# A four-layer graph attention kernel: order of emission, values by Strassen, lengths by a power

## The chip, the core and the metric

The kernel runs on one core of one Trainium2 chip. A core has five engines, each with its own queue of instructions: TensorE (PE, matrix products, results into PSUM), VectorE (DVE), ScalarE (ACT, functions by table and copies), GpSimd (POOL) and SyncE (SP, which here issues transfers). They run side by side and wait for one another by semaphores. The metric is the device time of one execution in microseconds (us), taken as the median of the runs.

## What is computed

128 graphs of 64 nodes with 512 features go through four layers. Each layer normalizes, applies ReLU, and adds the result of a masked attention to its input. Layers 0 and 2 have four heads of 64, layer 1 has eight and a second normalization. Layer 3 multiplies its attention by a second mask, the pairs of nodes whose cosine is over 0.1, and for this it needs the length of each head's vector at each node. The reference, cut:

```python
# layers 0 and 2 (x is the normalized input, 512 wide; q, k, v are 256 wide)
q, k, v = split_heads(x @ Wq), split_heads(x @ Wk), split_heads(x @ Wv)
sim = jnp.where(adjacency_mask[:, None], jnp.einsum('bhid,bhjd->bhij', q, k) * scale, neg)
out = jnp.einsum('bhij,bhjd->bhid', jax.nn.softmax(sim, axis=-1), v)   # then @ Wo + bo
# layer 1: the same with 8 heads, q, k, v and output 512 x 512
# layer 3
m = embs @ map_w.T + map_b
sem = m.reshape(b, s, h, dk).transpose(0, 2, 1, 3)
norm = jnp.maximum(jnp.linalg.norm(sem, axis=-1, keepdims=True), COS_EPS)
n = sem / norm
cos_adj = (einsum('bhsd,bhtd->bhst', n, n) * keep > THRESHOLD)
# q and k from m, softmax as above
adj = cos_adj * p_attn
Ax = jnp.einsum('hbst,hbtd->hbsd', adj_h, embs @ gcn_map_w.T + gcn_map_b)
out = jax.nn.relu(Ax @ gcn_W.T / (adj_h.sum(-1, keepdims=True) + 1.0))
```

## The kernel before

The work is cut into 16 steps of 512 rows (eight graphs) for each layer. The kernel is written as streams: Python generators that say, ahead of each instruction, which engine it needs and for how long (`yield act(0.6)` for 0.6 us of ScalarE). While the program is built, an object `Order` steps through all streams as if they ran, and emits each next instruction from the stream that could start first. These figures therefore decide the order in which instructions stand on each engine; they have no other effect. Buffers come from rings and banks, and a stream that asks for one waits until the earlier user has let go.

```python
def run(self):
    while self.live:
        ...
        s = min(self.live, key=lambda s: (s.start(self.free), s.prio))
        eng, dur, lat = s.op
        at = s.start(self.free)
        self.free[eng] = at + dur
        s.ready = at + dur + lat
        s.last = (eng, at + dur)
        self.step(s)
```

Almost all 512 x 512 products are done by Winograd's form of Strassen's method: both operands are cut into quarters, sums of quarters are made, and seven products of quarters take the place of eight. `A` holds the weights with their sums (made once by GpSimd), `B` the quarters of the tokens and `T` their sums (four GpSimd instructions a step). A product of quarters is four matmuls (two halves of 128, two steps of contraction). Three PSUM banks are used in turn; each product's result must be copied out or added before its bank takes the next:

```python
def product(bank, A, B, tokens_out, first):
    KC = A.shape[1]
    for m in range(2):
        o = bank[:, m * H:(m + 1) * H]                # H = 256
        for k in range(KC):
            yield pe(0.432)
            ...
            nc.tensor.matmul(o, l, r, ...)

def winograd(A, BT, tokens_out, out_, used, begun):
    ...                                               # "first": copy by ACT; "second": add by DVE
    mA = product(A[:, 0], B(0, 0)); read, c11 = first(0, 0, mA)
    mB = product(A[:, 1], B(1, 0)); c11 = second(0, 0, mB, c11)
    wait read;  mA = product(A[:, 5], T[:, 1]); read, u2 = first(0, 1, mA)
    mC = product(A[:, 4], T[:, 0]); read5, c22 = first(1, 1, mC)
    wait read;  mA += product(A[:, 2], T[:, 2]); read, c22 = add(1, 1, mA, c22)
    wait read5; mC += product(A[:, 6], B(1, 1)); c12 = second(0, 1, mC, u2)
    wait read;  mA += product(A[:, 3], T[:, 3]); alone(1, 0, mA)
```

(This last function is shortened to its order.) The values of layers 0 and 2 are the exception, plain products of 512 x 256:

```python
def v_proj(inT, w, t):
    n = w.shape[2]                                    # 256
    p_, e = yield from r_mm.new("mmv")
    for c in range(NC):                               # NC = 4
        yield pe(0.857 * n / 512)
        nc.tensor.matmul(p_[:, 0:n], inT[:, c, t * P:(t + 1) * P], w[:, c, :], ...)
    return p_[:, 0:n], e
...
for t in range(TB):                                   # TB = 4
    p_, e = yield from v_proj(h, v_part(W[f"vo{l}"]), t)
    od.spawn(evict(V[:, t, 0:D // 2], p_, e), 0)      # one copy by ACT
```

The lengths of layer 3 (the four rows of `mmn` matmuls sum the squares; only 8 of the 128 rows of `rs` are of use):

```python
def norms(mT, s, m_ready, ready, used):
    ...                                               # squares by ACT, sums by PE into p_
    nc.vector.tensor_scalar_max(rs, p_, 1e-16)
    nc.scalar.activation(rs, rs, AF.Sqrt)
    for h in range(4):
        v = rs[:, h * P:(h + 1) * P]
        nc.vector.reciprocal(v, v)
    nc.sync.dma_start(d, rs)                          # d is in DRAM
    for c in range(NC):
        for par in range(2):                          # each row spread over 64 partitions
            nc.sync.dma_start(t[par * N:(par + 1) * N, :], ...d[32 * c + par]...)
    yield used                                        # q and k of this step are done with mT
    for c in range(NC):
        nc.gpsimd.tensor_mul(mT[:, c, :], mT[:, c, :], t)
    ready.set()                                       # now the scores of mT with itself
```

Of the kernel before, what the change touches and what calls it, by code (L numbers as in the profile page):

```python
# [43 lines left out]

class Event:
# [38 lines left out]


class Order:


    def __init__(self):
        self.live, self.free, self.now, self.held = [], {}, 0.0, set()  # L90

# [28 lines left out]

    def run(self):
        while self.live:
            new = [s for s in self.live if s.op is None]
            if new:
                self.step(new[0])
                continue
            s = min(self.live, key=lambda s: (s.start(self.free), s.prio))
            eng, dur, lat = s.op
            at = s.start(self.free)
            self.free[eng] = at + dur  # L130
            s.ready = at + dur + lat
            s.last = (eng, at + dur)
            self.step(s)
        assert not self.held, [where(s.gen) for s in self.held]
# [51 lines left out]

def dve(us):
# [11 lines left out]
def load(us=2.2):  # L199
    return ("sp", 0.35, us)  # L200
# [3 lines left out]
def gnn_stack(ctx: ExitStack, tc: tile.TileContext, a: dict, out: bass.AP):  # L204
# [80 lines left out]
    def v_part(t):  # L285

        return t.rearrange("p a k n -> p (a k) n")[:, 0:4]

    def o_part(t):

        return t.rearrange("p a k n -> p (a k) n")[:, 4:11, None, :]

    def wo_halves(t, n):
# [4 lines left out]
             ("vo0", lambda t: [(a["Wv0"], v_part(t))] + wo_halves(t, "Wo0")),  # L298
# [3 lines left out]
             ("vo2", lambda t: [(a["Wv2"], v_part(t))] + wo_halves(t, "Wo2")),  # L302
             ("map3", lambda t: halves(t, "map3")), ("sem3", lambda t: []),
             ("q3", lambda t: halves(t, "q3")), ("k3", lambda t: halves(t, "k3"))]
    for key, _ in units:
        w_ready[key], w_sums[key] = od.event(), od.event()
    bo, bo_done = {}, {}

    def sums_of_a(A):

        for o, i0, i1, op in ((4, 2, 3, ALU.add), (5, 4, 0, ALU.subtract),
                              (6, 1, 5, ALU.subtract), (2, 0, 2, ALU.subtract)):
            yield pool(1.3)
            nc.gpsimd.tensor_tensor(A[:, o], A[:, i0], A[:, i1], op)

    def sums_of_b(B, T, vector=False):

        n = T.shape[2]
        for o, i0, i1 in ((T[:, 0], B(0, 1), B(0, 0)), (T[:, 1], B(1, 1), T[:, 0]),
                          (T[:, 2], B(1, 1), B(0, 1)), (T[:, 3], B(1, 0), T[:, 1])):  # L320
            if vector:
                yield dve(0.6 * n)
                nc.vector.tensor_tensor(o, i0, i1, ALU.subtract)
            else:
                yield pool(0.65 * n)
                nc.gpsimd.tensor_tensor(o, i0, i1, ALU.subtract)  # L326

    def weights():
        for key, parts in units:
# [17 lines left out]
            yield from sums_of_a(o_part(t) if key in ("vo0", "vo2") else t)  # L347
# [36 lines left out]
    def scales(v):  # L384
# [13 lines left out]
        yield dve(0.2)  # L398
# [4 lines left out]
    def normalize(v, rs, func):  # L403
        for t in range(2):
            yield act(0.69)
# [11 lines left out]
    def loads(steps):  # L417
        for l, s in steps:
            if l > 0:
                yield x_done[l - 1, s]  # L420
            for half in range(2):
                v, e = yield from r_xin.new()
                loaded[l, s, half] = v, e
                yield load()
# [80 lines left out]
    def product(bank, A, B, tokens_out, first):  # L505

        KC = A.shape[1]
        for m in range(2):
            o = bank[:, m * H:(m + 1) * H]
            for k in range(KC):  # L510
                yield pe(0.432)
                if tokens_out:
                    l, r = B[:, k, m * P:(m + 1) * P], A[:, k, :]
                else:
                    l, r = A[:, k, m * P:(m + 1) * P], B[:, k, :]
                nc.tensor.matmul(o, l, r, start=(first and m == 0 and k == 0),  # L516
                                 stop=(k == KC - 1), skip_group_check=True)

    class Out:
# [5 lines left out]
        def first(self, i, k, p_, read, done):  # L525
# [4 lines left out]
            else:  # L530
                for m in range(2):
                    yield act(0.45)
# [5 lines left out]
        def second(self, i, k, p_, after, done):  # L538
            yield after
            o = self.view(i, k)  # L540
            yield dve(0.69)
# [3 lines left out]
        def add(self, i, k, p_, after, read, done):  # L545
# [6 lines left out]
            yield dve(0.7)  # L552
# [3 lines left out]
        def alone(self, i, k, p_, done):  # L556
            yield from self.first(i, k, p_, done, od.event())

    def winograd(A, BT, tokens_out, out_, used, begun):

        B, T, *sums = BT

# [3 lines left out]
        def first(i, k, p_):  # L566
            read, done = ev(2)
            od.spawn(out_.first(i, k, p_, read, done), 0)
            return read, done

        def second(i, k, p_, after):
            done = od.event()
            od.spawn(out_.second(i, k, p_, after, done), 0)
            return done

        def add(i, k, p_, after):
            read, done = ev(2)
            od.spawn(out_.add(i, k, p_, after, read, done), 0)
            return read, done

        p_, pe_ = yield from r_ma.new("mA")
        yield from product(p_, A[:, 0], B(0, 0), tokens_out, True)
        read, c11 = first(0, 0, p_)
        q_, qe = yield from r_mm.new("mB")
        yield from product(q_, A[:, 1], B(1, 0), tokens_out, True)
# [7 lines left out]
        r_, re_ = yield from r_mm.new("mC")  # L593
        yield from product(r_, A[:, 4], T[:, 0], tokens_out, True)
# [11 lines left out]
        od.spawn(out_.alone(1, 0, p_, pe_), 0)  # L606
        od.spawn(when([c11, c12, c22, pe_], used), 0)
# [41 lines left out]
    def evict(o, p_, e):  # L649
        yield act(0.4)  # L650
        nc.scalar.copy(o, p_)
        e.set()

    def v_proj(inT, w, t):
        n = w.shape[2]
        p_, e = yield from r_mm.new("mmv")
        for c in range(NC):
            yield pe(0.857 * n / 512)
            nc.tensor.matmul(p_[:, 0:n], inT[:, c, t * P:(t + 1) * P], w[:, c, :],  # L659
                             start=(c == 0), stop=(c == NC - 1))  # L660
        return p_[:, 0:n], e

    st, p_ready, s_ready, p_used, with_ones = {}, {}, {}, {}, []

    def projections(steps):
        for l, s in steps:
# [4 lines left out]
            if l in (0, 2):  # L671
# [3 lines left out]
                od.spawn(when([used], s_ready[l, s], t_done[l, s],  # L675
                              w_done[f"qk{l}"] if end else None), 0)
# [3 lines left out]
                es = [used]  # L680
                for t in range(TB):
                    p_, e = yield from v_proj(h, v_part(W[f"vo{l}"]), t)
                    od.spawn(evict(V[:, t, 0:D // 2], p_, e), 0)
                    es.append(e)
                z["v"] = V
                od.spawn(when(es, p_ready[l, s], h_done[l, s]), 0)
# [73 lines left out]
    def norms(mT, s, m_ready, ready, used):  # L760
# [14 lines left out]
        rs, re_ = yield from r_u.new("rs")  # L775

        yield dve(0.69)
        nc.vector.tensor_scalar_max(rs, p_, 1e-16)
        pe_.set()
        yield act(1.9)  # L780
        nc.scalar.activation(rs, rs, AF.Sqrt)
        for h in range(4):
            v = rs[:, h * P:(h + 1) * P]
            yield dve(0.87)
            nc.vector.reciprocal(v, v)
        d = dram.tile([P, TB * P], F32, name=f"rs{s}")
        yield load()
        nc.sync.dma_start(d, rs)
        re_.set()
        nr = []  # L790
        for c in range(NC):
            t, e = yield from r_u.new("nr")
            yield ("sp", 0.35, 1.0)
            for par in range(2):
                v = d[32 * c + par:32 * c + par + 1, :]
# [13 lines left out]
    def scores(lT, rT, npair, blocks):  # L809
# [3 lines left out]
        for b, t in enumerate(blocks):  # L813
            for ch in range(nch):
                j = ch * nb + b
                yield pe(0.29)
# [55 lines left out]
    def masks(l, s):  # L872
# [3 lines left out]
        yield load()  # L876
# [22 lines left out]
    def residuals(l, s, w_there, got):  # L899
        yield w_there  # L900
        for k in range(2):
            xr, xe = yield from r_xres.new()
            yield load()
# [8 lines left out]
    class Residual(Out):  # L912
# [26 lines left out]
        def alone(self, i, k, p_, done):  # L939
            return self.second(i, k, p_, None, done)  # L940

    def store(l, s, done, got, evs):
# [3 lines left out]
        for k in range(2):  # L946
            xr, xe = got[k]
            yield load()
# [10 lines left out]
    def attention(l, s):  # L959
# [8 lines left out]
        for u, blocks in enumerate(units):  # L968
# [3 lines left out]
            for b, t in enumerate(blocks):  # L972
                for ch in range(nch):
                    j = ch * per + b
                    yield pe(0.29)
# [224 lines left out]
```

## Time and profile before

| | before |
|---|---|
| median of 3 runs | 2981.0 us |
| lowest and highest | 2978.83 and 2983.35 us |
| span of the profiled execution | 2978.9 us |
| instructions | 63888 |

The profile is of one execution. For each engine it gives busy time and its share of the span; PEld is the loading of weights, which overlaps the matmuls. A group of instructions is one line of code with its tiles and shapes: busy us, mean ns of one, then the idle us of the engine just before them and who ended that wait. An f32 matmul is two records, a transpose is one. The chain of work that ended last is followed back from the end, and tells whose time the span is. A timeline line has the start, the length, the engine, the line of code and the tiles, the number of instructions merged, and in brackets the idle time before and who ended it. A wait line has the total us, the number of times and the longest.

| group in the page's fifth part | count | busy us | mean ns |
|---|---|---|---|
| L659 PE, plain products of the values | 1024 records | 233.4 | 380 |
| L516 PE, mA from t and w_q, one of the groups of Strassen products | 768 records | 187.1 | 379 |
| L785 DVE, reciprocals of the lengths | 64 | 57.1 | 917 |
| L397 POOL, power of the normalization, 128x2 | 160 | 118.4 | 740 |
| L757 POOL, row of gcn added | 64 | 81.4 | 1305 |

(The third row is from the list of all groups.)

### The profile page before, as it was taken

To read this page: it belongs to the slowest core of one execution; us is meant where nothing else is said; L and a number is where in the kernel's file an instruction comes from. 1 tells how busy PE (TensorE), PEld (TensorE's weight loads), DVE (VectorE), ACT (ScalarE), POOL (GpSimd) and SP (SyncE) were. 2 spreads that over 40 slices of the span, in tenths; PEclk is the share of its full clock that TensorE was granted. 3 is DMA by queue.
4 is the path that set the end of the run, shared out by engine and by line. 5 is a ranking of instruction groups with operands and counts; after the bars stand their busy time and mean duration, and the time that the engine had idled before them with its cause. 6 is when DMAs were issued, how large, how long until landed. Compare 5 with 4: busy or idle time off the path is not lost.

```text
span 2978.9 us, 63888 instructions
## 1 busy us (share of the span) xinstructions
PE 2910.6 (98%) x27176; PEld 2468.1 (83%) x27176; DVE 1727.3 (58%) x2748; ACT 1336.6 (45%) x2361; POOL 1465.2 (49%) x1144
## 2 busy tenths in 40 slices
PE   8999999999999999999999999999999999999997
PEld 6888888888888888888888888887888787888876
DVE  5665566664554555445456556556666666665566
ACT  4444445544444444433444444454444444444442
POOL 6666667444344334335566566663344343344332
PEclk9999999999999999999999999999999999999998
DMA  5323333211112112113233332422232222222212
GB/s 163 116 88 123 95 101 126 67 62 66 48 45 73 59 44 73 59 44 98 94 114 104 102 116 88 138 82 64 72 90 83 63 62 66 70 85 71 52 48 62
DMA packets 162957, 244.05 MB, mean 82 GB/s; under 512 B 17392, under 2 KB 69616, under 8 KB 162672
## 3 DMA queue, kind: packets, MB, share of 16 engines
q1 hardware_dynamic: 149760, 226.56, 24.3%
q10 hardware_dynamic: 12912, 13.42, 1.4%
q8 instruction: 213, 3.49, 0.5%
q14 instruction: 72, 0.59, 0.1%
HBM read 168.60 MB, written 71.30 MB: 81 GB/s over the span
## 4 chain that ended last, share of the span: by engine, by line
PE 85%; DVE 6%; ACT 4%; DMA 2%; POOL 2%; issue 1%; SPq 0%; DVEq 0%; ACTq 0%; POOLq 0%
PE mA L516 37%; PE mC L516 18%; PE mB L516 10%; PE sc L824 4%; PE mmv L659 4%; PE ptp L864 3%; PE ptr L477 3%; PE po L983 2%; ACT E L846 1%; PE po L1118 1%; DVE E L843 1%; DVE sc L835 1%; DVE mx L840 1%; PE mmn L773 1%; PE ptr L454 1%
## 5 line engine op out<-in xcount | busy, mean ns | idle before, releaser
L853 POOL TENSOR_TENSOR E<-E,sm 128x1024 f32<-128x1024 f32 x96 | 186.3, 1941 | 424.2 <-DVE sm L851 298.7
L390 DVE BATCH_NORM_STATS2 st<-xin 128x6 f32<-128x512 f32 x320 | 215.6, 674 | 260.2 <-DMA xin<-x 206.9
L929 POOL TENSOR_TENSOR xres<-xres,u 128x512 f32<-128x512 f32 x192 | 243.4, 1268 | 250.0 <-ACT u L924 245.0
L908 POOL TENSOR_TENSOR xres<-xres,u 128x512 f32<-128x512 f32 x192 | 257.7, 1365 | 219.5 <-DMA xres<-x 99.6
L406 ACT ACTIVATE xin<-xin,rs 128x512 f32<-128x512 f32 x320 | 243.7, 808 | 110.9 <-DVE rs L399 110.7
L397 POOL TENSOR_TENSOR rs<-rs,mhalf 128x2 f32<-128x2 f32 x160 | 118.4, 740 | 276.9 <-DVE rs L395 270.3
L659 PE MATMUL mmv<-w_vo,hT 128*128 128x256 f32 x1024 | 233.4, 380 | 0.9 <-DVE xres L542 0.9
L659 PEld LDWEIGHTS mmv<-w_vo,hT 128*128 128x128 f32 x1024 | 193.5, 190 | 29.0 <-DVE xres L542 2.6
L326 POOL TENSOR_TENSOR t<-hT 128x512 f32<-128x512 f32 x128 | 178.3, 1393 | 73.2 <-ACT hT L482 39.0
L326 POOL TENSOR_TENSOR t<-hT,t 128x512 f32<-128x512 f32 x128 | 172.3, 1346 | 50.5 <-ACT hT L459 46.6
L399 DVE SCALAR_TENSOR_TENSOR rs<-mv,rs 128x2 f32<-128x2 f32 x160 | 80.3, 502 | 197.7 <-POOL rs L397 197.7
L516 PE MATMUL mA<-t,w_qk 128*128 128x256 f32 x768 | 187.0, 380 | 2.8 <-ACT qk L529 2.5
L516 PE MATMUL mA<-t,w_k 128*128 128x256 f32 x768 | 182.7, 381 | 4.8 <-ACT kT L533 4.7
L516 PE MATMUL mA<-t,w_q 128*128 128x256 f32 x768 | 187.1, 379 | 0.0
L516 PEld LDWEIGHTS mA<-t,w_k 128*128 128x128 f32 x768 | 144.8, 190 | 28.2 <-ACT kT L533 8.3
L516 PEld LDWEIGHTS mA<-t,w_qk 128*128 128x128 f32 x768 | 143.1, 190 | 22.0 <-ACT qk L529 3.3
L868 ACT COPY pt<-ptp 128x512 f32<-128x512 f32 x192 | 112.7, 588 | 105.1 <-PE ptp L864 105.1
L516 PEld LDWEIGHTS mA<-t,w_q 128*128 128x128 f32 x768 | 143.1, 190 | 18.1
L849 DVE TENSOR_REDUCE sm<-E 128x16 f32<-128x1024 f32 x96 | 116.4, 1212 | 69.5 <-ACT E L846 69.5
L757 POOL TENSOR_TENSOR v<-v,gcn_row 128x512 f32<-128x512 f32 x64 | 81.4, 1305 | 150.4 <-ACT v L615 150.4
L482 ACT COPY hT<-ptr 128x512 f32<-128x512 f32 x192 | 113.7, 592 | 74.1 <-PE ptr L477 74.1
L846 ACT ACTIVATE E<-E 128x1024 f32<-128x1024 f32 x96 | 101.5, 1058 | 83.6 <-DVE E L843 83.3
(210 smaller groups left out, 6819.0 us busy)
## 6 DMA issues: line engine op xcount, KB each, us to landing
x<-xres SPq DMA_DIRECT2D x96, 512.0 KB, 3.8
xin<-x SPq DMA_DIRECT2D x96, 512.0 KB, 3.8
xres<-x SPq DMA_DIRECT2D x64, 512.0 KB, 4.2
xin<-in_x SPq DMA_DIRECT2D x32, 512.0 KB, 3.8
xres<-in_x SPq DMA_DIRECT2D x32, 512.0 KB, 4.6
u<-rs SPq DMA_DIRECT2D x128, 128.0 KB, 3.1
xres<-x SPq DMA_DIRECT2D x256, 64.0 KB, 2.3
out<-xres SPq DMA_DIRECT2D x256, 64.0 KB, 2.1
```

The lines of the kernel that those rows point to most:

```text
L326: nc.gpsimd.tensor_tensor(o, i0, i1, ALU.subtract)
L390: nc.vector.bn_stats(st, v[:, t, :])
L397: nc.gpsimd.tensor_tensor(rs[:, 0, :], rs[:, 1, :], mhalf[:, :2], ALU.pow)
L406: nc.scalar.activation(v[:, t, :], v[:, t, :], func, bias=rs[:, 2, t:t + 1], scale=rs[:, 0, t:t + 1])
L516: nc.tensor.matmul(o, l, r, start=(first and m == 0 and k == 0), stop=(k == KC - 1), skip_group_check=True)
L659: nc.tensor.matmul(p_[:, 0:n], inT[:, c, t * P:(t + 1) * P], w[:, c, :], start=(c == 0), stop=(c == NC - 1))
L824: nc.tensor.matmul(S[a_ * N:(a_ + 1) * N, par, col], lT[r, c, k], rT[r, c, k], start=True, stop=True)
L846: nc.scalar.activation(E, E, AF.Exp, scale=0.125)
L849: nc.vector.tensor_reduce(sm, E, AX.X, ALU.add)
L853: nc.gpsimd.tensor_mul(E, E, sm[:, :, None].to_broadcast([P, 16, N]))
L908: nc.gpsimd.tensor_add(xr[:, t, :], xr[:, t, :], bo[l])
L929: nc.gpsimd.tensor_add(v, v, both(u))
```

## The change

It has three parts. First, the values of layers 0 and 2 are computed by the same seven products as the rest, with quarters of the weights 128 columns wide; `v_proj` and its copy go. This is meant to take multiplications away. Second, the lengths of layer 3: the eight useful rows of sums go to DRAM and come back as 128 x 32, GpSimd raises them to the power -0.5, they go to DRAM and are spread as before. This takes away the root, whose table ACT has to load in place of that for Exp, and the reciprocals of 512 columns. Third, the order of emission: the assumed times are corrected, a change between 64-row matmuls ("quads") and full ones is charged 0.085 us, and a long ACT or DVE instruction of low priority gives way to an urgent one that could start within its time. Also the transfers at the end of layer 3 are written as two of 128 KB where there were four of 64 KB. The diff, cut to its core:

```diff
+DRAIN = 0.085
 class Order:
+    def urgent(self, s):
+        eng, end = s.op[0], s.start(self.free) + s.op[1] - 0.1
+        if s.prio <= 0 or eng not in ('act', 'dve'):
+            return None
+        r = [x for x in self.live if x.prio <= 0 and x.op is not None and x.op[0] == eng
+             and x.start(self.free) < end]
+        return min(r, key=lambda x: x.start(self.free), default=None)
     def run(self):
             s = min(self.live, key=lambda s: (s.start(self.free), s.prio))
-            eng, dur, lat = s.op
+            s = self.urgent(s) or s
+            eng, dur, lat = s.op[:3]
             at = s.start(self.free)
+            if eng == "pe":
+                at += DRAIN * (self.quads != s.quads())
+                self.quads = s.quads()
...
 def load(us=2.2):
-    return ("sp", 0.35, us)
+    return ("sp", 0.6, us)
...
     def normalize(v, rs, func):
-            yield act(0.69)
+            yield act(0.81)
...
     def product(bank, A, B, tokens_out, first):
-        KC = A.shape[1]
+        KC, n = A.shape[1], bank.shape[1] // 2
-            o = bank[:, m * H:(m + 1) * H]
+            o = bank[:, m * n:(m + 1) * n]
-                yield pe(0.432)
+                yield pe(max(0.219, 0.432 * n / H))
...
     def winograd(A, BT, tokens_out, out_, used, begun):
+        width = 2 * A.shape[3] if tokens_out else 2 * H
...                                                   # "used" now waits for every eviction
     def projections(steps):
-                for t in range(TB):
-                    p_, e = yield from v_proj(h, v_part(W[f"vo{l}"]), t)
-                    od.spawn(evict(V[:, t, 0:D // 2], p_, e), 0)
-                    es.append(e)
+                def vv(i, k, V=V):
+                    return V[:, 2 * k:2 * k + 2, i * P:(i + 1) * P]
+                es = [used, (yield from unit(v_part(W[f"vo{l}"]), (*BT, wv_sums[l]), True, Out(vv)))]
-                od.spawn(when(es, p_ready[l, s], h_done[l, s]), 0)
+                od.spawn(when(es, p_ready[l, s], t_done[l, s], h_done[l, s]), 0)
...
     def norms(mT, s, m_ready, ready, used):
-        nc.vector.tensor_scalar_max(rs, p_, 1e-16)
-        yield act(1.9)
-        nc.scalar.activation(rs, rs, AF.Sqrt)
-        for h in range(4):
-            v = rs[:, h * P:(h + 1) * P]
-            yield dve(0.87)
-            nc.vector.reciprocal(v, v)
-        nc.sync.dma_start(d, rs)
+        nc.vector.tensor_copy(ss, p_)
+        for c in range(NC):
+            nc.sync.dma_start(d[0][2 * c:2 * c + 2, :], ss[32 * c:32 * c + 2, :])
+        nc.sync.dma_start(rs, d[0].rearrange("h (k n) -> (h k) n", n=32))
+        nc.vector.tensor_scalar_max(rs, rs, 1e-16)
+        yield pool(6.0)
+        nc.gpsimd.tensor_tensor(rs, rs, mhalf[:, 0:1].to_broadcast([P, 32]), ALU.pow)
+        nc.sync.dma_start(d[1].rearrange("h (k n) -> (h k) n", n=32), rs)
...
     def scores(lT, rT, npair, blocks):
-                yield pe(0.29)
+                yield quads(0.235)
```

## The prediction

> **What bounds the kernel now.** I read the page's first two parts, then the chain, then the busy times by stage, then the timeline around waits of TensorE (PE). The stretches of the third fence are, roughly, layers 0 to 3.
>
> ```profile
> PE 2910.6 (98%) x27176; PEld 2468.1 (83%) x27176; DVE 1727.3 (58%) x2748; ACT 1336.6 (45%) x2361; POOL 1465.2 (49%) x1144
> PEclk9999999999999999999999999999999999999998
> ```
> ```profile
> PE 85%; DVE 6%; ACT 4%; DMA 2%; POOL 2%; issue 1%; SPq 0%; DVEq 0%; ACTq 0%; POOLq 0%
> ```
> ```profile
> 0.00:520.00 520.00, 498.37 (x4327) 426.35 (x4328) 309.75 (x511) 246.00 (x423) 337.17 (x276) 1.00 0.36 115
> 520.00:1470.00 950.00, 944.13 (x8471) 820.37 (x8469) 500.06 (x838) 419.84 (x649) 403.96 (x318) 1.00 0.20 66
> 1470.00:1955.00 485.00, 479.61 (x4130) 412.22 (x4131) 277.45 (x430) 223.07 (x397) 304.45 (x243) 1.00 0.31 105
> 1955.00:2979.00 1024.00, 988.48 (x10252) 809.14 (x10250) 640.06 (x970) 447.65 (x893) 419.60 (x310) 0.99 0.25 69
> ```
>
> The columns after the length of a stretch are busy us of PE, its weight loads, DVE, ACT and POOL. PE is the bound in every layer, at full clock; no other engine passes 70% of a stage. So only two things count: PE work taken out, and PE waits. Work saved on DVE, ACT, POOL or DMA counts only through such a wait.
>
> PE's real waits are partly inside its busy time. Matmul records start 0.216 us apart but last 0.38, so a wait under 0.16 us is not idle and a longer one shows 0.16 short. This is a wait in layer 3, PE first, then ACT at the same moment:
>
> ```profile
> 2252.72 1.89 PE L516 MATMUL mA<-t,w_map 128*128 128x256 f32 x8
> 2255.18 1.99 PE L516 MATMUL mC<-hT,w_map 128*128 128x256 f32 x8 [0.57 <-ACT m L533]
> ```
> ```profile
> 2252.05 1.28 ACT L846 ACT_TABLE_LOAD   x1
> 2253.34 1.06 ACT L846 ACTIVATE E<-E 128x1024 f32<-128x1024 f32 x1
> 2254.30 0.82 ACT L533 ACTIVATE m<-mC,vecs 128x256 f32<-128x256 f32 x2
> ```
>
> Eight records at 0.216 should have brought the next start at 2254.45; it came at 2255.18, 0.73 us late (0.57 shown). ACT copied bank mC late because it had reloaded a table for Exp, just as long as the wait could bear. The whole list of PE's waits for ACT begins:
>
> ```profile
> PE mC L516 <- ACT m L533: 8.6, 15, 0.6
> PE mC L516 <- ACT u L924: 6.2, 16, 0.5
> PE mA L516 <- ACT kT L533: 4.7, 4, 1.2
> ```
>
> With 0.16 us added to each, that is 11.0, 8.8 and 5.3 us. The three are most of what can be gained in the steady state; the start (first PE work at 9.69 us) and the last 20 us hold the rest.
>
> [...]The trace has two records of 0.216 us for one f32 matmul of 256 columns[...]; the groups show 16 loads at Sqrt and 16 at Exp of layer 3, 1283 ns each.[...]
>
> **Part 1, values by Strassen (layers 0 and 2).** Removed: 512 matmuls of 256 columns (16 for each of 32 steps), the 1024 records of this group:
>
> ```profile
> L659 PE MATMUL mmv<-w_vo,hT 128*128 128x256 f32 x1024 | 233.4, 380 | 0.9 <-DVE xres L542 0.9
> ```
>
> At start-to-start pace 1024 x 0.216 = 221 us (233.4 counts tails). Added: seven products of four matmuls, 28 x 32 = 896, each 128 columns wide; the built program has exactly these counts. Does such a matmul take half, or does loading 128x128 weights for only 128 columns bind? The fold of the weights, in the middle of the kernel, has that shape:
>
> ```profile
> 1492.74 0.81 PE L659 MATMUL mmv<-w_vo,hT 128*128 128x256 f32 x3
> 1493.39 1.05 PE L377 MATMUL mmf<-bdw,bb 128*128 128x128 f32 x8
> 1494.28 1.43 PE L659 MATMUL mmv<-w_vo,hT 128*128 128x256 f32 x5
> ```
>
> Eight records from 1493.39 to 1494.28: 0.89 us, 0.111 each, 0.222 for a matmul. So weight loads do not bind, and 896 x 0.222 = 199 us. PE saves 221 - 199 = 22 us.
>
> What it adds elsewhere: ACT has five 128x256 copies for four, at 0.37 us (47.0 us / 128 in the old group), +12 us; DVE has two adds from PSUM and one from SBUF a step, which layer 3's same lines show at 0.40 and 0.53 us, 32 x 1.33 = +43 us; POOL forms four weight sums of half width in each of the two layers, and holds T longer. All off the bound. The new danger is that a bank is reused after shorter products. In the new order mA is reused after a product on mC (0.89 us) and mostly a matmul of another unit (0.43): 1.3 us for tail (0.16), copy (0.37) and handover. That is enough unless ACT is inside a long instruction (Exp 1.06, output copy 1.01, normalize 0.81). I estimate 0.2 us a step, +6 us in all.
>
> **Part 2, lengths by a power.** Removed: 64 reciprocals (57 us of DVE), 16 roots (10 us) and, what matters, both table loads of each step, since Exp's table now stays. Without the 1.28 us before Exp, the copy of mC in the fence above comes 1.28 us earlier, against a wait of 0.73. The order of the map unit is otherwise unchanged there. Gain 11 us.
>
> Added: a trip to DRAM and back before the power, and the power on 128x32. The only power in the trace is small:
>
> ```profile
> L397 POOL TENSOR_TENSOR rs<-rs,mhalf 128x2 f32<-128x2 f32 x160 | 118.4, 740 | 276.9 <-DVE rs L395 270.3
> ```
>
> If nothing of the 0.74 us is fixed, 32 columns take 11.8 us; the scheduler's own figure in the changed source is 6.0. Is it on the path? In the step shown, the rows of gcn are added until 2227.2 on POOL, the lengths are first used by the scores of m at 2257.97, and the order puts the power right after these rows. After it come a store (about 2.8), eight broadcast reads (about 5 to issue, 3.1 to land: the page's DMA part) and four products of 5.4 in sum: 2227.2 + power + 16.3 = 2243.5 + power. So a power up to some 14 us costs nothing. Net 0.
>
> **Part 3, order of emission.** Both builds have the same 505 changes between 64-row and full-size PE work, so the new drain charge saves none. It does move work: in the output units of layers 0 and 2, mC's second use stood after one product (0.86 us) and waited for ACT's copy:
>
> ```profile
> 314.52 1.03 PE L516 MATMUL mA<-w_vo,t 128*128 128x256 f32 x4
> 316.05 1.13 PE L516 MATMUL mC<-w_vo,m 128*128 128x256 f32 x4 [0.51 <-ACT u L924]
> ```
>
> It now has a matmul of the next step in between, 1.3 us. I count 8 of 8.8 us. The rule that puts evictions ahead of other long work on ACT should take some of the kT waits, 4 of 5.3, and a few small waits at the removed matmuls, 2. I give back 5 us for waits that the order makes elsewhere and that I can't see.
>
> **Sum.** -22 (PE work) + 6 (V banks) - 11 (table loads) - 8 - 4 - 2 + 5 (order) = -36. 2981 - 36 = 2945 us, ratio 0.988.
>
> **Rivals.**
> *The V units stall.* Products of 0.89 us on three banks could each wait 0.3 us for ACT or DVE; at three a step that is 29 us instead of 6, and the time 2968. For: ACT and DVE get 55 us more in these layers, in the same moments. Against: 1.3 us between uses, and ACT below 50%.
> *The power is long.* At 20 us it passes the room of 14 by 6 us, sixteen times: +96 and 3041. For: 0.74 us for two columns is very slow. Against: even taken wholly as per-column it stays at 11.8.
> *Only arithmetic counts.* The new order brings nothing and the table wait is replaced by another: 2981 - 22 + 6 = 2965.
> *The order does more.* All three listed waits vanish, nothing new comes, and the end shortens by some us: 2981 - 22 - 25 - 8 = 2926.
>
> **Range and chances.** The arithmetic (-22) is nearly sure; the waits are not, each way by some 15 to 20 us. Eight in ten: 2924 to 2966. Faster by over 2% means below 2921.4, which needs more than every listed wait: 0.07. Slower by over 2% (above 3040.6) needs the long power or a broken pipeline: 0.03. Within 2%: 0.90.
>
> **What would show it.** PE records 27,944; 128-column records about 0.111 us apart; one table load left for Exp in the whole layer 3; no waits of mC at map for ACT m; waits at w_vo near zero; layer 1's pace of 57.0 us a step unchanged; a step of layer 0 some 1.2 us and of layer 3 some 0.8 us shorter. Wrong if scores of m wait for POOL's m products, if the power is over 14 us, or if new waits of mA and mC for ACT v sum to over 20 us.

## The result and the profile after

| | before | after |
|---|---|---|
| median | 2980.59 us (4 runs) | 2936.85 us (4 runs) |
| lowest and highest | | 2935.35 and 2939.24 us |
| span of the profiled execution | 2978.9 us | 2933.6 us |
| ratio after / before | | 0.9853, 95% interval 0.9836 to 0.987 |

The changed kernel is 44 us faster, 8 us beyond the 2945 predicted and inside the range. Its busy times and the engines of its chain of waits:

```profile
PE 2866.9 (98%) x27944; PEld 2485.4 (85%) x27944; DVE 1841.6 (63%) x2796; ACT 1321.5 (45%) x2345; POOL 1582.1 (54%) x1168
```
```profile
PE 93%; DVE 3%; POOL 1%; issue 1%; ACT 0%; DMA 0%; SPq 0%; DVEq 0%; POOLq 0%
```

Of the chain, 93% is now PE's (85% before), and ACT's 4% are gone. By layer (columns as before; the layers now end earlier, so the borders are at 510, 1460 and 1940 us):

```profile
0.00:510.00 510.00, 484.37 (x4691) 432.86 (x4692) 330.90 (x540) 257.20 (x431) 349.79 (x276) 0.99 0.35 117
510.00:1460.00 950.00, 946.33 (x8516) 823.96 (x8515) 541.49 (x860) 428.89 (x660) 406.37 (x328) 1.00 0.19 66
1460.00:1940.00 480.00, 479.19 (x4549) 429.74 (x4549) 300.36 (x481) 237.85 (x419) 309.81 (x245) 1.00 0.31 106
1940.00:2933.00 993.00, 957.04 (x10193) 798.88 (x10191) 668.87 (x917) 397.57 (x835) 516.12 (x321) 0.99 0.24 68
```

PE is still the bound everywhere. In layer 3 POOL has some 100 us more (the powers) and ACT 50 less. The map unit, where the prediction's example waited, PE first and then ACT:

```profile
2535.72 1.89 PE L550 MATMUL mA<-t,w_map 128*128 128x256 f32 x8
2537.44 1.89 PE L550 MATMUL mC<-hT,w_map 128*128 128x256 f32 x8
```
```profile
2534.92 1.06 ACT L883 ACTIVATE E<-E 128x1024 f32<-128x1024 f32 x1
2535.92 0.84 ACT L571 ACTIVATE m<-mC,vecs 128x256 f32<-128x256 f32 x2
```

No table load stands before Exp (the trace has one in all, 1.28 us at 5.85 us), and the second product on mC starts 1.72 us after the one before it, which is eight records at 0.216: no wait at all. The list of PE's waits, without its small entries:

```profile
PE ptr L511 <- ACT xin L440: 18.4, 3, 9.6
PE ptp L901 <- DVE E L1127: 11.7, 14, 0.9
...
PE mA L550 <- ACT u L961: 3.1, 1, 3.1
```

All three waits that headed the prediction's list (mC for m, mC for u, mA for kT) are gone; the wait of the transposes `ptp` for DVE is new.

A sum of my own from the trace shows where the time went. For every pair of neighbouring PE records I took the usual start-to-start time of such a pair and summed what was over it by more than 30 ns. The stretches are the same in both traces, but for the border at 500 us, which is at 490 in the changed kernel, whose change to layer 1 begins there:

| stretch, us | waits before | waits after |
|---|---|---|
| 0 to 100, start | 10.7 | 12.3 |
| 100 to 500, layer 0 | 12.8 | 3.0 |
| 500 to 600, change to layer 1 | 5.7 | 12.6 |
| 600 to 1400, layer 1 | 5.3 | 5.8 |
| 1400 to 1900, mostly layer 2 | 15.8 | 10.4 |
| 1900 to 60 us before PE's last record | 51.7 | 40.0 |
| last 60 us of PE | 15.4 | 10.1 |
| sum | 117.5 | 94.2 |

By this sum waits fell by 23.3 us. Of these, 3.7 us are no waits: the sum also counts the time in which one group of `mmn` records runs before the next (13.7 us before, 10.0 after). So waits fell by some 20 us. With the 22 us of multiplication that the prediction counted out, this makes 42 of the 48.0 us by which PE's last record starts earlier (at 2971.86 us before, at 2923.88 after); what follows that record takes 2.6 us longer, so the spans differ by 45.3. The remaining 6 us, net, are work of PE in another order, and the largest piece of it is in layer 3. A step's `mmn` matmuls, two groups before and one after:

```profile
2457.18 1.05 PE L773 MATMUL mmn<-u,sel 128*32 128x512 f32 x2
2458.74 1.06 PE L773 MATMUL mmn<-u,sel 128*32 128x512 f32 x6
```
```profile
2422.78 1.06 PE L805 MATMUL mmn<-u,sel 128*32 128x512 f32 x8
```

Whether two, six or eight of these records stand together, they take 1.05 or 1.06 us here. In the new order they stand in one group in 15 of 16 steps, where they stood in two. With the waits taken off, a step in the middle of layer 3 is 60.2 us long instead of 61.25 (means of seven steps). The prediction has no term for this.

The clearest single measure is the pace: the time from a unit's first mB product in one step to that in the next, in the steady part of a layer. It will carry most of the verdicts below.

| kernel | step of layer 0 | step of layer 3 | median ratio |
|---|---|---|---|
| before | 30.6 to 31.7 | 63.6, some 64.8 | 1 |
| Strassen alone | 27.9 to 33.2, by turns | 63.6 | 1.0003 |
| lengths alone | 30.5 to 31.7 | 65.9 to 67.8 | 1.0097 |
| both, old order | 28.0 to 33.3, by turns | 65.6 to 68.8 | 1.0088 |
| order alone | 30.55 | 63.61 | 0.9963 |
| order and lengths | 30.55 | 62.54 | 0.9895 |
| order and Strassen | 29.59 | 63.61 | 0.9895 |
| after (all three) | 29.59 | 62.53 | 0.9853 |

Layer 1 has 56.96 to 57.01 us in before and after, as predicted.

### The profile page after: what moved, and what is told of

It reads as the page before. It is cut to its first block, busy times and chain, and to the rows that moved or that the text cites. A ratio compares the mean times of both kernels' runs of the same rounds, so it can differ in the third digit from the quotient of the medians.

```text
span 2933.6 us, 65553 instructions
## 1 busy us (share of the span) xinstructions
PE 2866.9 (98%) x27944; PEld 2485.4 (85%) x27944; DVE 1841.6 (63%) x2796; ACT 1321.5 (45%) x2345; POOL 1582.1 (54%) x1168
## 4 chain that ended last, share of the span: by engine, by line
PE 93%; DVE 3%; POOL 1%; issue 1%; ACT 0%; DMA 0%; SPq 0%; DVEq 0%; POOLq 0%
PE mA L550 45%; PE mC L550 23%; PE mB L550 10%; PE sc L861 5%; PE ptp L901 3%; PE ptr L511 3%; PE po L1020 2%; PE po L1154 1%; DVE E L1127 1%; PE ptr L488 1%; DVE Cf L1121 1%; PE mmn L805 1%; POOL xres L966 0%; DVE sc L872 0%; POOL t L356 0%
## 5 line engine op out<-in xcount | busy, mean ns | idle before, releaser
L966 POOL TENSOR_TENSOR xres<-xres,u 128x512 f32<-128x512 f32 x192 | 242.4, 1270 | 243.0 <-ACT u L961 235.2
L945 POOL TENSOR_TENSOR xres<-xres,u 128x512 f32<-128x512 f32 x192 | 281.4, 1488 | 102.1 <-DMA xres<-in_x 78.7
L440 ACT ACTIVATE xin<-xin,rs 128x512 f32<-128x512 f32 x320 | 253.4, 813 | 48.3 <-DVE rs L433 47.7
L550 PE MATMUL mA<-w_vo,t 128*128 128x128 f32 (+1 forms) x1152 | 203.9, 311 | 3.1 <-ACT u L961 3.1
L356 POOL TENSOR_TENSOR t<-hT,t 128x512 f32<-128x512 f32 x128 | 180.8, 1413 | 42.3 <-ACT hT L493 38.2
L550 PE MATMUL mA<-t,w_q 128*128 128x256 f32 x768 | 194.2, 382 | 0.0
L356 POOL TENSOR_TENSOR t<-hT 128x512 f32<-128x512 f32 x128 | 170.7, 1333 | 42.4 <-ACT hT L516 26.5
L550 PEld LDWEIGHTS mA<-w_vo,t 128*128 128x128 f32 x1152 | 169.7, 191 | 17.0 <-ACT u L961 5.0
L567 ACT COPY v<-mA 128x256 f32<-128x256 f32 (+1 forms) x144 | 63.8, 443 | 253.4 <-PE mA L550 229.6
L433 DVE SCALAR_TENSOR_TENSOR rs<-mv,rs 128x2 f32<-128x2 f32 x160 | 79.7, 498 | 109.3 <-POOL rs L431 109.2
L961 ACT COPY u<-mA 128x512 f32<-128x512 f32 x144 | 84.3, 585 | 128.1 <-PE mA L550 127.4
```

The source lines that it names most:

```text
L440: nc.scalar.activation(v[:, t, :], v[:, t, :], func, bias=rs[:, 2, t:t + 1], scale=rs[:, 0, t:t + 1])
L945: nc.gpsimd.tensor_add(xr[:, t, :], xr[:, t, :], bo[l])
L966: nc.gpsimd.tensor_add(v, v, both(u))
```

## The experiments

Three runs do one part alone, three do two parts, the rest undo or double one suspect. Medians are of four to six runs, of 20 for Strassen alone; the kernel before was run beside each group on its chip (2982.9, 2983.3 and 2984.5 us), so ratios are compared, not microseconds of different groups.

**Strassen alone.** The kernel before, with part 1 and its streams; old assumed times, old order rule, old lengths.

```diff
-units: ("vo0", [(Wv0, v_part)] + wo_halves)   # v_proj, evict
+units: ("vo0", wv_halves + wo_halves)         # unit(v_part(...), (*BT, wv_sums[l]), True, Out(vv))
```

> The kernel before with the values of layers 0 and 2 by Strassen, all other assumed times and the lengths as before. Theory (the parts add up; PE work is 22 us less, short banks cost some 6): 16 us less than before, 2965. Rival (the shorter products wait for ACT and DVE in the old order as much as they save): within 5 us of before. Second rival (all of the 44 us gained comes with this part): 2940.

2983.83 us, ratio 1.0003 (0.9995 to 1.0011): nothing gained. The 22 us of multiplication are out, and PE waits 25.8 us longer by the start-to-start sum. The two lines that head its list:

```profile
PE mA L526 <- ACT u L940: 17.2, 26, 2.3
PE mB L526 <- DVE xres L556: 14.9, 12, 1.8
```

One such moment in layer 0, on PE, DVE and ACT:

```profile
308.95 1.05 PE L526 MATMUL mA<-w_vo,hT 128*128 128x128 f32 x8
311.53 1.16 PE L526 MATMUL mB<-w_vo,hT 128*128 128x128 f32 x8 [1.53 <-DVE xres L556]
```
```profile
308.53 1.22 DVE L409 SCALAR_TENSOR_TENSOR rs<-mv,rs 128x2 f32<-128x2 f32 x1 [5.02 <-POOL rs L407]
309.67 1.22 DVE L851 COPY_PREDICATED sc<-n,negs 128x1024 f32<-128x1024 uint8 x1
310.80 0.68 DVE L556 TENSOR_TENSOR xres<-mB,xres 128x512 f32<-128x512 f32 x1
```
```profile
309.78 1.52 ACT L416 ACTIVATE xin<-xin,rs 128x512 f32<-128x512 f32 x2 [3.92 <-DVE rs L409]
311.20 0.56 ACT L940 COPY u<-mA 128x512 f32<-128x512 f32 x1
```

Read them from the bracket of DVE backwards. DVE stood 5.02 us at a small instruction of the next step's normalization, which waited for GpSimd's power; the addition that frees bank mB stood behind it in DVE's queue, and the copy that frees mA stood behind the normalization in ACT's. Products of 0.89 us come back to the banks sooner, so PE ran into both. What lay in wait was not the copies' length, which the prediction weighed, but a late instruction of other work ahead of them. The rival held, and so did "the V units stall" of the prediction, in the old order.

**Lengths alone.** The kernel before with the new `norms` only.

```diff
-nc.scalar.activation(rs, rs, AF.Sqrt)         # and 4 reciprocals
+nc.gpsimd.tensor_tensor(rs, rs, mhalf[:, 0:1].to_broadcast([P, 32]), ALU.pow)   # 128x32, by DRAM
```

> The kernel before with the lengths by the power alone. Theory (the table load ahead of Exp was what held up the copy of bank mC in the map unit, 15 x 0.73 us): 11 us less, 2970, and the wait of mC for ACT m gone. Rival (that wait is taken over by another[...]): within 4 us of before.

3010.67 us, ratio 1.0097 (1.0078 to 1.0116): slower. The wait for m at map is gone, as expected, and another took its place:

```profile
PE mA L516 <- ACT kT L533: 29.0, 10, 3.4
```
```profile
2383.70 1.89 PE L516 MATMUL mC<-t,w_k 128*128 128x256 f32 x8
2387.89 2.57 PE L516 MATMUL mA<-t,w_k 128*128 128x256 f32 x8 [2.31 <-ACT kT L533]
2390.25 3.05 PE L516 MATMUL mC<-m,w_k 128*128 128x256 f32 x8
```
```profile
2385.60 1.52 ACT L406 ACTIVATE xin<-xin,rs 128x512 f32<-128x512 f32 x2 [4.32 <-DMA xres<-x]
2387.03 0.81 ACT L533 ACTIVATE kT<-mA,vecs 128x256 f32<-128x256 f32 x2
```

```profile
2378.57 1.08 SPq L425 DMA_DIRECT2D xin<-x  x2
```
```profile
2382.68 0.69 DVE L390 BATCH_NORM_STATS2 st<-xin 128x6 f32<-128x512 f32 x1 [4.99 <-DMA xin<-x]
```

The same pattern with another origin. SP issued the load of the next step's xin only at 2378.57, behind broadcasts of the lengths and stores of the output, and DVE waited 4.99 us for it. The normalization of that xin ended ACT's idle 4.32 us (the bracket there names another load, of xres), and the copy of kT, whose bank PE wanted, stood behind it. The power itself takes 5.4 us in 15 of 16 steps, and no wait of PE names it. The third PE line shows a second cost: after the wait the same eight records last 3.05 us instead of 1.89. In the stretch from 2387.8 to 2391.0 the granted clock is 0.71. Counting both: 34.4 us of such waits start to start, against 5.3 before, 9.5 us of records at half pace, less 11 at map: +27.6, where the medians have +28. The prediction's "net 0" for what lengths add holds for GpSimd, and not for the queues that they share.

**Both, in the old order.** The two edits above together.

> The kernel before with Strassen and lengths, old order and old assumed times. Strassen is in layers 0 and 2 and lengths in layer 3, so they can hardly meet: their sum, 0 + 28, gives 3011 (3003 to 3019), with the waits of both single runs. Rival: the order of each build is reshuffled by any change, the waits of the single runs are chance, and this falls anywhere between 2960 and 3040 with other waits.

3010.17 us, ratio 1.0088 (1.0073 to 1.0103), with the waits of both single runs (mA for kT 27.1 us, mA for u 17.9, mB for xres 14.8). The sum 0 + 28 held: these two parts do not help each other.

**Order alone.** The changed kernel with plain values and with root and reciprocals put back.

```diff
-es = [used, (yield from unit(v_part(...), (*BT, wv_sums[l]), True, Out(vv)))]
+for t in range(TB): p_, e = yield from v_proj(...); od.spawn(evict(...), 0)
-nc.gpsimd.tensor_tensor(rs, rs, mhalf..., ALU.pow)
+nc.scalar.activation(rs, rs, AF.Sqrt)         # and 4 reciprocals
```

> The kernel after without the Strassen values and without the power: the new assumed times, the urgent rule, the drain charge and the 128 KB transfers are left. Theory (parts add): the rest of the 44 us, 44 - 16 - 11 = 17 less than before, 2964, with the waits of mC for ACT u and of mA for ACT kT gone. Rival (the order gains only together with the others, because table loads stay and the start of this order costs 8 us): within 5 us of before.

2971.1 us, ratio 0.9963 (0.995 to 0.9976), 11 us less. The waits for u at w_vo and for kT are gone, the wait for m at map stays (8.6 us in 15, the table is still loaded), and `ptp` for DVE's E comes in with 15.7 us, or 1.34 us in each steady step, start to start. So the pace of layer 3 stays at 63.61, although the `mmn` matmuls already stand in one group. The gain lies between what the theory and the rival expected.

**Order and lengths; order and Strassen.** The changed kernel with one part put back each.

> The changed kernel with the plain products of the values back, so order and lengths without Strassen. If the parts add to what they took alone (lengths +28, order -12), this should be near 2997 us. If the new order frees the lengths of their kT waits, which is the theory, the lengths bring about the 11 us of the map waits: 2960, between 2954 and 2966, and the trace has no kT waits over 2 us in sum. The theory's numbers for the changed kernel then leave 23 us to Strassen in the new order.

> The changed kernel with the root and the reciprocals back, so order and Strassen without the lengths. If Strassen is worth nothing because banks are held whatever the order, this stays at the 2971 of the order alone. Theory: in the new order the 22 us of work come out whole, 2949 (2944 to 2955), the waits at w_vo sum to under 8 us, and the wait of mC at map, about 8.6 us in 15, remains.

2953.51 us, ratio 0.9895 (0.9881 to 0.991), and 2952.66 us, ratio 0.9895 (0.988 to 0.991): the first half a microsecond below its range, the second inside. In the new order the lengths bring 20 us where they cost 28 in the old, and there are no kT waits; Strassen brings 20 where it brought nothing. Against the kernel with all three, each part is worth 12 to 13 us by the ratios, 18 and 16 us by the profiled spans. What the two parts take from each other is thus 1.5 us by the spans and at most 7 by the ratios, whose intervals don't resolve it. The paces of the table show the same without the noise of medians: Strassen takes 0.96 us from each step of layer 0, with lengths or without; lengths take 1.08 from each step of layer 3, with Strassen or without. In the steady part they add exactly. Strassen's 0.96 us in each of 32 steps would be 31 us in all, where the kernels show 18 to 20. The larger part of the difference is lost at one place, with or without the lengths: the change from layer 0 to layer 1. Summed as in the table of stretches, from 480 to 600 us, PE waits there 2.5 and 3.0 us in the two kernels of the new order without Strassen, and 10.8 and 12.9 in the two with it, where mA waits for ACT's u (2.3 and 3.1 us) and `ptp` for GpSimd's E (2.8 and 2.9).

**The table put back.** The changed kernel, with a root of one column in each step of layer 3, so that ACT loads two tables a step again.

```diff
+yield act(1.9)
+nc.scalar.activation(one, mhalf[:, 1:2], AF.Sqrt, scale=-1.0)    # result not used
```

> The kernel after with a root of one column put back in each step's lengths, its result unused: two table loads a step return, 2 x 1.28 us on ACT, and nothing else. Theory (the loads mattered because one stood ahead of Exp and so ahead of the copy that PE waits for): up to 11 us more than after, 2948, with 0.7 us waits of mC at map. Rival (the urgent rule now puts the copy ahead of Exp, so the loads no longer matter): within 3 us of after, 2937.

```profile
PE mC L550 <- ACT m L571: 8.0, 14, 0.6
PE ptp L904 <- DVE E L1130: 7.3, 16, 0.8
```

2938.59 us, ratio 0.9856 (0.9841 to 0.9872). The wait came back whole, 14 times 0.73 us start to start, so its cause is shown. The pace of layer 3 rose by only 0.37 us, to 62.90, since the wait of `ptp` for E shrank (11.7 to 7.3 us, in a steady step from 1.06 to 0.63): PE, held at map, asked later for E. Two waits in one loop overlap, and taking one away uncovers the other. In the median of the whole kernel the two loads a step can't be told from none, as the rival expected, but not for its reason: the copy of m still stands behind Exp.

**No urgent rule.**

```diff
-            s = self.urgent(s) or s
```

> The kernel after without the rule that lets an urgent eviction go ahead of a long ACT or DVE instruction; all assumed times stay. Theory (the corrected transfer times are what makes the parts fit, since late inputs put normalizations in front of evictions on ACT): at most 6 us more than after, up to 2943. Rival (the rule itself takes the waits away): 20 us or more above after, 2957 or more, with waits of PE for ACT u, v and kT as in the two parts run alone.

```profile
PE mA L549 <- ACT kT L586: 33.8, 10, 4.0
```

2973.68 us, ratio 0.9968 (0.9951 to 0.9985), by the ratios 34 us slower than the changed kernel. The rival held, and nearly all of it is this one line of PE's waits in layer 3. That is the wait of the lengths alone, back again.

**Old assumed times of transfers.** The changed kernel, with all loads and stores that go by `load` assumed as before; the figures of the lengths' own transfers stay.

```diff
-    return ("sp", 0.6, us)      # callers: 2.3 to 4.6
+    return ("sp", 0.35, us)     # callers: 2.2
```

> The kernel after with the assumed times of transfers as before (0.35 us of queue and 2.2 us to land for all loads and stores); the urgent rule and all other assumed times stay. Theory: 25 us or more above after, 2962 or more, with PE waiting for ACT u or v in layers 0 and 2 and for ACT kT in layer 3, and the inputs of the normalization issued late in layer 3. Rival (the urgent rule suffices): within 6 us of after.

```profile
PE sc L861 <- ACT qk L567: 13.8, 15, 1.7
PE mA L550 <- ACT v L567: 7.4, 17, 2.5
```

2967.84 us, ratio 0.995 (0.9933 to 0.9967), by the ratios 29 us slower, as the theory said. Here layer 3 keeps its 62.54, without the expected waits for kT; layer 2 slows to 30.5 to 32 us a step and layer 0 becomes uneven. So these two pieces of the new order serve different layers: the rule protects layer 3, the assumed times of transfers protect Strassen in layers 0 and 2. The other new times, the charge for changes and the transfers of 128 KB were not tried one by one. The times are figures in the source with no effect but on the order.

**The power twice.** Two powers in the slot of one, the first result not used.

```diff
+        nc.gpsimd.tensor_tensor(r2, rs, mhalf[:, 0:1].to_broadcast([P, 32]), ALU.pow)
```

> The kernel after with each power of 128x32 done twice (once into an unused tile) within the same assumed time, so 12.8 us instead of 6.4 on GpSimd. Theory (prediction: a power of up to some 14 us is hidden): within 4 us of after. Rival (GpSimd's order behind it, the sums of tokens, the normalization's power and the products of m, is already tight): 6.4 us more in each of some 12 to 15 steps, 60 us or more above after.

```profile
PE mA L550 <- ACT kT L571: 8.8, 10, 1.6
```

```profile
2516.68 5.42 POOL L826 TENSOR_TENSOR rn<-rn,mhalf 128x32 f32<-128x32 f32 x1
2527.63 0.70 POOL L431 TENSOR_TENSOR rs<-rs,mhalf 128x2 f32<-128x2 f32 x1
```
```profile
2528.36 0.16 DVE L433 SCALAR_TENSOR_TENSOR rs<-mv,rs 128x2 f32<-128x2 f32 x1 [4.46 <-POOL rs L431]
```
```profile
2528.56 1.52 ACT L440 ACTIVATE xin<-xin,rs 128x512 f32<-128x512 f32 x2 [2.81 <-DVE rs L433]
2529.99 0.82 ACT L571 ACTIVATE kT<-mA,vecs 128x256 f32<-128x256 f32 x2
```

2947.06 us, ratio 0.9881 (0.9866 to 0.9895): by the ratios 8 us slower, ten steps of layer 3 at 63.6 instead of 62.5. The prediction's room of "some 14 us" counted the way of the lengths to the scores of m. The time is lost on another way: the small power of the next step's normalization stands on GpSimd behind the second long one and the sums of tokens that follow it, the normalization comes late, and the copies of kT stand behind it on ACT. Neither theory's number was met.

**Times mended.** The changed kernel with two assumed times raised: the product E * Cf to 2.3 us, which takes 2.25 or 2.26 us in 12 of its 32 cases in the changed kernel's trace, and the landing of weights from 10 to 11 us, a figure of the source and not a measured one. In the trace the first sums of weights start at 12.91 us, 9.96 us after the issue of the load that they wait for.

```diff
-            yield dve(1.22)     # E * Cf
+            yield dve(2.3)
-                yield ("actq", 1.0, 10.0)
+                yield ("actq", 1.0, 11.0)
```

> The kernel after with two assumed times mended: the product of E with the cosine mask on DVE 2.3 us (it takes 2.25 where GpSimd works beside it, and PE's transposes wait 1.06 us for it in 12 steps of layer 3), and the landing of weights 11 us instead of 10 (at the start the sums of weights stand ahead of the power of the second half step and PE idles 8.25 us). Theory: both waits go, 12 + 6 = 18 us less than after, 2919. Rival (the order moves the waits elsewhere): within 5 us of after.

2933.91 us, ratio 0.9843 (0.9826 to 0.986). Both waits went (3.6 us left of `ptp` for E, 10.7 of 18.4 us at the start), but layer 3's pace is 62.65: the 1.06 us a step of the wait did not turn into time, because this order puts the `mmn` matmuls in two groups again, with transposes between:

```profile
2418.09 1.06 PE L805 MATMUL mmn<-u,sel 128*32 128x512 f32 x6
2419.08 0.66 PE L901 MATMUL ptp<-ident,E 128*128 128x128 f32 x4
2419.67 1.05 PE L805 MATMUL mmn<-u,sel 128*32 128x512 f32 x2
```

With the waits taken off, a steady step is 61.3 us long instead of 60.2: what the wait gave, the order took back in PE's own work. A wait of 8.0 us for GpSimd's sums of w_k came in at the beginning of layer 3. Eighteen us were expected, and about three came, less than the intervals resolve.

**Times mended, last weights as before.**

```diff
-                yield ("actq", 1.0, 11.0)
+                yield ("actq", 1.0, 10.0 if key == "k3" else 11.0)
```

> The run with mended times, but the last weights of layer 3 assumed to land after 10.0 us, as in the changed kernel, so that their fourth sum stands with the other three ahead of the next tokens' sums on GpSimd. If the 8.0 us wait for that sum was on the path, the time is 2926 (2923 to 2929). Rival: the order after that point is another one and brings waits of its own, so 2930 to 2937 as before.

2932.13 us, ratio 0.9828 (0.9811 to 0.9844), which on a kernel before of 2981 is 2930. The wait for w_k's sums is gone and those for DVE's y at the very end rose from 2.7 to 5.9 us. This is the lowest time of the study, but its interval meets those of the run above and of the changed kernel, so that it beats the latter is likely, not shown.

## Why the prediction was right, and where not

**The bound and the two things that count: right.** Multiplications and waits make 42 of PE's 48 us. The rest, the `mmn` matmuls in one group above all, is also PE work taken out, but not by any part of the sum. PE's 27,944 records are as predicted. The step of layer 3 is 1.04 us shorter than the 63.57 before, and that of layer 0 by 1.0 to 2.1, against 0.8 and 1.2 predicted.

**Strassen's multiplications, -22: right, and undersized together with its waits.** In the new order the step of layer 0 is 0.96 us shorter by Strassen, 0.69 of it (22 / 32) multiplication. The other 0.27 are small waits: they sum to 0.61 us a step without Strassen in the new order and to 0.30 with it. The term "V banks, +6" thus has the wrong sign in the steady part of the new order, and the 8 to 10 us at the change to layer 1 are in no term; in the old order it would have been +26. The mechanism that I named for it, ACT inside a long instruction, was too small a picture: ACT and DVE stood idle, waiting, at the head of their queues.

**Table loads, -11: the wait right, its gain half of that, and another gain of the lengths not seen.** The wait is gone and came back on demand, 0.73 us each. But the two loads account for 0.37 us a step, some 6 us in 15 steps, and lengths as a whole take 1.08 (16 us). The other 0.71 is PE's wait for DVE's E: in a steady step it is 1.34 us with the root and the reciprocals and 0.63 with the loads alone. Whether the root, the reciprocals or the order around them lengthens that wait was not tried.

**The power, net 0: right for 6.4 us, wrong for the room.** The estimate of 6.0 to 11.8 us held:

```profile
L824 POOL TENSOR_TENSOR rn<-rn,mhalf 128x32 f32<-128x32 f32 x16 | 99.6, 6222 | 4.3 <-DVE rn L822 4.2
```

At twice the length 1.07 us a step is lost where I had counted on 14 us of room. I had followed one user of the power; the next instruction in its queue was the other.

**Order, -8 -4 -2: right in the steady state.** The waits for u and for kT are gone, in the changed kernel and in the three that put back part 1, part 2 or both, but for one wait for u of 2 to 3 us at the change to layer 1 where Strassen is in.

**New waits, +5: too small by what can be seen, and made up for.** `ptp` for E is 11.7 us, the start has one of 8.25, the layer change 5 to 7 more than before. The first, on PE, DVE and GpSimd:

```profile
2502.75 0.27 PE L511 MATMUL ptr<-ident,xin 128*128 128x128 f32 x1
2503.91 0.63 PE L901 MATMUL ptp<-ident,E 128*128 128x128 f32 x4 [0.89 <-DVE E L1127]
```
```profile
2501.51 2.25 DVE L1127 TENSOR_TENSOR E<-E,Cf 128x1024 f32<-128x1024 f32 x1
```
```profile
2498.09 4.60 POOL L789 TENSOR_TENSOR v<-v,gcn_row 128x512 f32<-128x512 f32 x4
2502.64 6.41 POOL L824 TENSOR_TENSOR rn<-rn,mhalf 128x32 f32<-128x32 f32 x1
```

In the three of its 32 cases with no GpSimd instruction beside it, E * Cf takes 1.22 or 1.23 us. Here it starts within GpSimd's last row addition, ends 1.07 us after that addition's end, and takes 2.25 us, about 1.0 us more. The order had assumed 1.22. In the start, GpSimd's sums of the first weights (5.16 us, from 12.91) stand ahead of the power of a normalization, and PE has nothing else to do; but the kernel before lost nearly as much in its first 100 us in smaller pieces, so this costs 1.6 us net. What covered the rest is not in the prediction either: the 1.04 us a step that the `mmn` matmuls in one group save in layer 3, as much as the new wait for E costs there, and smaller waits in layers 0, 2 and at the end. That these cancel so nearly is luck.

**What failed is the sum as such.** It adds three independent parts. Measured alone, they are 0, +28 and -11, which is +17; together they are -44. The working took the waits of the old order and struck those that each part removes, and did not ask what stands ahead of each eviction (the copy or addition that frees a bank) in the queues of ACT, DVE and SP once PE is faster or a transfer is added. Within the new order the terms are of about the predicted size, and that is why the total was near: order -11 for the predicted -9, then Strassen -20 or -12 for -16, then lengths -12 or -20 for -11. Part of that nearness is luck, too: the banks that were to cost 6 us, the small waits that went and the change to layer 1 cancel in Strassen, and half a gain at map and an unseen one at E make up the lengths. The rival "the order does more" was the nearest of the four, and the truth went further: the order is what makes the other two worth having.

## What to carry to other kernels

Before counting the gain of faster work on the bound engine, look at each copy or addition that frees its buffers and ask what stands ahead of it in its queue, and when that is ready: a late instruction of other work there cost 25 to 35 us in three of these kernels, while PE's list for the changed kernel has one wait of a Strassen product for such a copy, of 3.1 us. In a kernel ordered by assumed durations, measured durations of transfers and a rule for urgent evictions can decide whether another change pays, so a change should be tried in the order that it will run in. A wait is worth only its distance to the next wait of the same loop: 0.73 us put back cost 0.37. And a new order also changes what the bound engine's own work takes: 1.06 us of wait removed brought nothing, because the same reordering made that work 1.1 us longer.

## What the hardware showed that was not expected

*Some DVE and GpSimd instructions took longer beside each other.* In the trace of the changed kernel the scale-and-shift of the normalization, 128x2 (L433), takes 0.10 to 0.16 us in 106 cases, in 93 of them with no GpSimd instruction beside it, and 1.22 in the median of the other 54, each of which ends 15 to 22 ns after a GpSimd instruction does. E * Cf (L1127) takes 1.22 or 1.23 us in 4 of its 32 cases and 1.45 to 2.26 in the other 28, each with GpSimd instructions beside it. Not every DVE instruction is longer: the mask Cf just ahead of it (L1121) takes 1.22 or 1.23 us in all 32 cases, 29 of them with GpSimd at work. GpSimd's side shows it too: the power takes 5.41 or 5.42 us in 3 steps and 6.40 or 6.41 in 13, and in each of these 13, as in the moment shown, DVE was inside E * Cf when the power began.

*After some PE waits the records came at half pace.* In the lengths alone, after seven of the kT waits, of 2.5 to 3.6 us, records came 0.427 us apart instead of 0.216, six to eight of them in a row; after three others of 2.5 to 3.2 us none did. In the moment shown there the granted clock is 1.00 from 2383.0 to 2385.5 us, ahead of the wait, and 0.71 from 2387.8 to 2391.0, after it. The changed kernel has such a moment at the change to layer 1: after the wait of 3.13 us for u the granted clock is 0.56 from 504.2 to 508.0 us, and seven records in a row come 0.426 or 0.427 us apart. What tells the waits with a slow stretch after them from those without was not shown.
